# A masked graph layer: bf16 in three parts on 96 rows, and float32r in two parts on 32-row tiles

## The chip, the cores and the metric

The kernel runs on one core of a Trainium2 chip. A core has TensorE (PE, the matrix engine), VectorE (DVE), ScalarE (ACT), GpSimd (POOL) and SyncE (SP, which here only issues transfers). Each has its own queue of instructions and works it off in order; semaphores tie them together. TensorE multiplies a stationary operand (loaded first, "LDWEIGHTS" or PEld) with a moving one that is streamed column by column, and leaves the sums in PSUM, a memory of eight banks with 512 float32 columns in each of 128 partitions. The other engines read PSUM ("drain" it) and work in SBUF. The metric is device time in microseconds; lower is better.

## The reference

There are 128 graphs of 128 nodes with 64 features, and for each graph an adjacency matrix that is mostly zero (about 12% of its entries are positive, the diagonal among them).

```
h   = max(layernorm(x), 0)
mask = adj > 0
hm[j] = sum over k with mask[j,k] of relu(h[j] @ W1a + (h[j] - h[k]) @ W1b + b1)   # 192 units
x   = x + hm @ W2 + deg * b2
h   = max(layernorm(x), 0)
x   = x + (adj @ h) @ W.T
```

The heavy part is the sum over neighbours. It splits into a node part and a centre part: relu(c[k] + a[j]) with c = -h @ W1b and a = h @ (W1a + W1b) + b1. Only the pairs (j, k) that the mask allows count.

## The kernel before

**Groups.** The graphs are worked off in 32 groups of four (`G = 4`). For a group, `pre_...` functions prepare, `Job`s do the slot products, and `edge_...`, `slot_sum` and `post0` to `post4` finish. While the jobs of group g run, the preparation of group g+1 and the finish of group g-1 are put between them.

**Slots.** The 128 nodes k are cut into four quarters (`Q = 4`) of 32. In each quarter a centre j gets up to `D = 6` slots, one for each neighbour there; neighbours beyond that go to an overflow list of up to 128 edges per graph (`edge_x`, `edge_sum`, `edge_sum1`). `pre_rank` gives each neighbour its number in its quarter, and `pre_slots` makes the one-hot S: S[k, d, j] is 1 where k is slot d of j. A product of S with the node parts c puts c[k] into (d, j); a product of an identity with the centre parts adds a[j] to it. Unused slots then hold relu(a[j]) alone, which the term z takes off again.

**Parts.** `pre_proj` projects two graphs at a time into PSUM (float32 products into the tile `pp`, with a bf16 product for the biases) and splits the result exactly into three bf16 parts: ScalarE copies the first (`ca<-pp`), VectorE subtracts (`rest`), ScalarE copies the second (`ca<-rest`), POOL subtracts for the third. A slot product has to add the three parts, so they are stacked: `pre_stack` copies each quarter's 32 rows of each part to 96 rows (k3, twelve copies of 96 KB), and S is copied to three times 32 rows as well (S3, twelve copies of 192 KB at the end of `pre_slots`). In group 0 S3 is made in place by `first_ranks` and `first_slots`.

**Jobs.** A `Job` takes one double bank of PSUM (`gtile`, a pool of three double banks; `pre_proj` takes its `pp` from the same pool; the small tiles have the other two banks). It handles two quarters for one half (64) of the centres. Kind 0, called wide here, handles units 0 to 127 of one graph: two node products of 384 columns and four centre products of 192. Kind 1, called narrow, handles units 128 to 191 of two graphs, 64 rows of output for each, and so twice as many products on half the array. There are 16 wide and 8 narrow jobs in a group. The drain of a wide job is one VectorE reduction (`hm<-g`, sum of absolute values over slots); a narrow one is a Relu on ScalarE (`T<-g`) and additions on POOL.

**Order.** TensorE's order is the program's (`mm` and `tp` keep it; they are lines 181 and 184 in the profile): job by job, and behind each job the pieces that the tables OWN, BEHIND and AHEAD name for it. The other engines' instructions go through a wrapper (line 198) that holds the program order only until the main loop; there the framework's scheduler orders them by its own priorities. Every copy between partitions is issued on SP.

Of the kernel before, what the change touches and what calls it, by code (L numbers as in the profile page):

```python
# [9 lines left out]
BF16 = mybir.dt.bfloat16  # L10
I32 = mybir.dt.int32
# [139 lines left out]
def kernel(  # L151
# [67 lines left out]
    K3 = 3 * QN  # L219
# [8 lines left out]
    with ExitStack() as main:  # L228
# [41 lines left out]
        triq = const.tile([P, P], BF16, tag="triq", name="triq")  # L270
        vec.memset(triq, 0.0)
# [3 lines left out]

        triq3 = tmp.tile([P, Q, 3, QN], BF16, tag="u0", name="triq3", bufs=1)
        for part in range(3):
            vec.tensor_copy(
                triq3[:, :, part], triq.rearrange("p (q j) -> p q j", q=Q)
            )  # L280
# [5 lines left out]

        rks = const.tile([P, D, G * N], BF16, tag="rks", name="rks")
        for i in range(D):
            pool.memset(rks[:, i], float(i) + BIG)

        mident = const.tile([P, P], F32, tag="mident", name="mident")
        identb = const.tile([P, P], BF16, tag="identb", name="identb")

        id32 = const.tile([P, QN], F32, tag="id32", name="id32")
        id3 = const.tile([P, QN], BF16, tag="id3", name="id3")
# [3 lines left out]
        def constants():  # L299
            vec.tensor_scalar(mident, ident, -1.0, None, ALU.mult)  # L300
            vec.tensor_copy(identb, ident)
            vec.tensor_reduce(
                id32, ident.rearrange("p (q j) -> p j q", q=Q), AX.X, ALU.add
            )
            vec.tensor_copy(id3, id32)
            vec.tensor_copy(upb, upper)
            vec.tensor_scalar(ioe, iov, BIG, None, ALU.add)
# [13 lines left out]

        def weight_loads():
            act.dma_start(w2a, W2[0:C0, :])
            act.dma_start(b1c, b1[0:C0].unsqueeze(1))
            act.dma_start(bias[:, 0:H], b1.unsqueeze(0).to_broadcast([P, H]))
            act.dma_start(b2s, b2.unsqueeze(0).to_broadcast([P, O]))
            for p in range(2):
                s = slice(p * F, (p + 1) * F)
                sp.dma_start(w1[s], W1.rearrange("(t f) h -> f t h", t=2))
# [16 lines left out]
        def weights_b():  # L346
# [3 lines left out]
            pw = mtile("pw")  # L350
            tp(pw[:, 0:P], wab[:, 0:C0], ident)
            vec.tensor_tensor(bias[:, H : H + O], pb[:, 0:O], b2s, ALU.add)
            vec.tensor_scalar(wp[:, 0:H], w1[:, 1], -1.0, None, ALU.mult)
            vec.tensor_copy(wT, pw[:, 0:P])
# [27 lines left out]
        groups: dict[int, dict] = {}  # L382

# [38 lines left out]
        def pre_adj(g):  # L422
# [8 lines left out]
            d["maskT"] = grp.tile([P, G, N], BF16, tag="maskT", name=f"maskT{g}")  # L431
# [23 lines left out]
        def pre_slots(g, first, last):  # L455

            d = groups[g]
            if first == 0:
                d["S"] = one.tile([P, D, G * N], BF16, tag="S", name=f"S{g}")
            n = last - first  # L460
            vec.tensor_tensor(
                d["S"][:, first:last], bc(d["qs"].rearrange("k b j -> k (b j)"), n, 1),
                rks[:, first:last], ALU.is_equal,
            )
            if last < D:
                return
            d["S3"] = grp.tile([K3, Q, D, G * N], BF16, tag="S3", name=f"S3{g}")
            for q in range(Q):
                for part in range(3):
                    sp.dma_start(  # L470
                        d["S3"][part * QN : (part + 1) * QN, q],
                        d["S"][q * QN : (q + 1) * QN],
                    )

        def first_ranks(g, qp):

            d = groups[g]
            pk = gtile(f"pk{g}_{qp}")
            if qp == 0:
                d["q3"] = tmp.tile([K3, Q, G * N], BF16, tag="T", name=f"q3{g}", bufs=3)  # L480
            for i in range(2):
                q = 2 * qp + i
                mm(
                    pk[0:K3, i], triq3[:, q].rearrange("k t j -> k (t j)"),
                    d["maskT"].rearrange("k b j -> k (b j)"), start=True, stop=True,
                )
            act.activation(d["q3"][:, 2 * qp : 2 * qp + 2], pk[0:K3], AF.Copy)

        def first_slots(g, q):

            d = groups[g]
            if "S3" not in d:
# [534 lines left out]
```

## Time and profile before

| | |
|---|---|
| runs | 1012.18, 1013.48, 1016.25 us, median 1013.48 |
| profiled execution | span 1013.2 us; no time of its own is listed beside the span |
| TensorE busy, weight loads busy | 963.8 us (95%), 721.6 us (71%) |
| VectorE, ScalarE, POOL busy | 799.7 us (79%), 704.1 us (69%), 765.9 us (76%) |
| granted TensorE clock, mean | 0.980 |
| DMA | 129.94 MB, 128 GB/s in the mean |
| S copies / k copies | 372 of 192 KB / 384 of 96 KB |

The page gives each engine's busy time in the span and then groups of instructions by line, engine and tile: busy time in all, the mean of one in ns, and the idle time just before them with what ended it. A tile's name stands for all its buffers: g is a job's double bank, S the one-hot, k the stacked parts, id the identity, hm and T the drains' results, pp the projection, pe and px the overflow edges. Because matmuls overlap in the pipeline, the time between the starts of two of them says more than their durations. The view of TensorE in order of time merges neighbours of the same kind ("x4") and gives start, length from the first start to the last end, and what they are.

### The profile page before, as it was taken

The numbers are of one execution on the slowest core, as the hardware profiler recorded it, in microseconds if no ns is written. First come the engines' busy times: TensorE is split into PE (matmuls) and PEld (weight loads), VectorE is DVE, ScalarE is ACT, GpSimd is POOL, SyncE is SP. The second block draws the span as 40 slices with busy tenths as digits, with TensorE's granted clock in tenths as the row PEclk, the third lists the DMA queues.
The fourth block names the chain that finished last, engine by engine and source line by source line (L and its number), as shares of the span: only waits on it lengthen the run. The fifth ranks groups of instructions, "written<-read, shape, count | busy, mean of one in ns | idle before, by whom it ended". The sixth has DMA issues, their size and how long they took to land.

```text
span 1013.2 us, 27270 instructions
## 1 busy us (share of the span) xinstructions
PE 963.8 (95%) x10314; PEld 721.6 (71%) x10314; DVE 799.7 (79%) x1769; ACT 704.1 (69%) x1732; POOL 765.9 (76%) x1134
## 2 busy tenths in 40 slices
PE   3899999999999999999999999999999999999996
PEld 2577777777777777777777777777767777777774
DVE  7767888777888877788877788877787877788863
ACT  5557876677777667777667787667786667787652
POOL 3278777787877777877778877777877778877783
PEclk9599999999999999999999999999999999999998
DMA  3526655556755556766555766545765555765420
GB/s 83 133 68 162 147 135 130 123 124 154 161 136 134 122 120 140 163 136 138 126 123 129 162 144 136 131 112 128 162 140 133 127 120 132 162 147 119 110 67 14
DMA packets 88296, 129.94 MB, mean 128 GB/s; under 512 B 47200, under 2 KB 63968, under 8 KB 88160
## 3 DMA queue, kind: packets, MB, share of 16 engines
q1 hardware_dynamic: 87584, 127.98, 55.2%
q8 instruction: 83, 1.36, 0.5%
q14 instruction: 53, 0.43, 0.1%
q10 hardware_dynamic: 576, 0.16, 0.1%
HBM read 13.01 MB, written 4.19 MB: 17 GB/s over the span
## 4 chain that ended last, share of the span: by engine, by line
PE 45%; DVE 25%; ACT 14%; DMA 5%; POOL 4%; issue 3%; SPq 2%; DVEq 1%; POOLq 0%; ACTq 0%
PE g L181 24%; DVE hm L198 9%; PE pe L181 8%; DVE S L198 8%; DMA k<-ca 4%; ACT ca L198 3%; PE px L181 3%; DVE u L198 3%; ACT et L198 3%; POOL T L198 3%; SPq L198 2%; PE pp L181 2%; PE py L181 2%; ACT h L198 2%; ACT T L198 2%
## 5 line engine op out<-in xcount | busy, mean ns | idle before, releaser
L198 POOL TENSOR_TENSOR T<-T 128x192 f32<-128x192 f32 (+2 forms) x768 | 543.6, 714 | 139.0 <-ACT T L198 99.1
L181 PEld LDWEIGHTS <-k 96*128 96x128 bf16 (+1 forms) x6144 | 412.4, 104 | 208.5 <-issue 87.4
L198 DVE TENSOR_REDUCE hm<-g 128x64 f32<-128x768 f32 x512 | 472.1, 948 | 110.4 <-PE g L181 108.6
L181 PE MATMUL g<-S,k 96*128 96x384 bf16 (+1 forms) x2048 | 392.1, 333 | 29.2 <-DMA k<-ca 14.3
L181 PE MATMUL g<-id,k 96*128 96x192 bf16 (+1 forms) x4096 | 384.1, 248 | 0.0
L198 ACT ACTIVATE T<-g 128x768 f32<-128x768 f32 x256 | 209.8, 821 | 48.5 <-PE g L181 48.5
L198 POOL TENSOR_TENSOR ca<-rest,ca 128x384 bf16<-128x384 f32 x126 | 114.0, 924 | 82.3 <-ACT ca L198 72.0
L198 ACT ACTIVATE ca<-pp 128x768 bf16<-128x768 f32 x64 | 51.3, 802 | 63.9 <-PE pp L181 63.9
L198 DVE TENSOR_TENSOR S<-qs,rks 128x1024 bf16<-128x1024 bf16 x93 | 86.9, 962 | 0.1
L198 ACT ACTIVATE hT<-ph 128x256 f32<-128x256 f32 x32 | 12.3, 383 | 104.0 <-PE ph L184 104.0
L181 PE MATMUL pe<-RT,X 128*64 128x128 f32 (+1 forms) x512 | 74.9, 285 | 0.0
L181 PE MATMUL pe<-mident,z 128*64 128x128 f32 (+1 forms) x512 | 68.8, 274 | 0.0
L181 PE MATMUL pp<-wp,hT 64*128 64x448 f32 x256 | 68.7, 614 | 0.0
L198 ACT ACTIVATE z<-pp,ns 128x128 f32<-128x128 f32 (+1 forms) x256 | 65.7, 347 | 0.0
L198 ACT ACTIVATE ca<-rest 128x768 bf16<-128x768 f32 x64 | 55.2, 863 | 11.6 <-DVE rest L198 11.6
L198 DVE TENSOR_TENSOR rest<-pp,ca 128x768 f32<-128x768 f32 x64 | 60.7, 948 | 3.2 <-ACT ca L198 3.1
L198 DVE TENSOR_SCALAR maskT<-adjT 128x512 bf16<-128x512 f32 x32 | 17.2, 538 | 52.7 <-PE pe L181 52.7
L198 ACT ACTIVATE et<-et,half 128x128 f32<-128x128 f32 x128 | 56.8, 449 | 0.0
L181 PEld LDWEIGHTS pe<-mident,z 128*64 128x64 f32 (+1 forms) x512 | 53.8, 164 | 0.0
L181 PEld LDWEIGHTS pe<-RT,X 128*64 128x64 f32 (+1 forms) x512 | 52.8, 164 | 0.1
L181 PE MATMUL px<-ca,S 128*128 128x192 bf16 x384 | 52.7, 246 | 0.0
L181 PE MATMUL px<-ca,R 128*128 128x192 bf16 x384 | 52.6, 246 | 0.0
(128 smaller groups left out, 1263.1 us busy)
## 6 DMA issues: line engine op xcount, KB each, us to landing
S<-S SPq DMA_DIRECT2D x372, 192.0 KB, 4.0
k<-ca SPq DMA_DIRECT2D x384, 96.0 KB, 2.2
adj<-in_adj_dram SPq DMA_DIRECT2D x32, 256.0 KB, 3.0
x<-in_x_dram SPq DMA_DIRECT2D x32, 128.0 KB, 2.7
out_dram<-ot SPq DMA_DIRECT2D x32, 128.0 KB, 2.2
w<-in_L_gnn_W_dram SPq DMA_DIRECT2D x2, 96.0 KB, 5.1
bias<-in_L_gnn_b_dram ACTq DMA_DIRECT2D x1, 96.0 KB, 4.6
w2a<-in_L_gnn_W_dram ACTq DMA_DIRECT2D x1, 32.0 KB, 2.2
```

Source lines behind the costliest of these rows:

```text
L181: return tc.keep_in_program_order(nc.tensor.matmul(*args, **kw))
L198: ins = f(*args, **kw)
```

## The change

The projection is split in two float32r parts in place of three bf16 parts. float32r is a 4-byte form of float32 with a shorter mantissa. ScalarE copies the first part (once for the node half, once for the centre half) and VectorE's subtraction writes the second; the third part on POOL and the second copy on ScalarE go. The parts lie in two tiles `cas` that the groups use in turn, each with a block of zeros between the two graphs' node parts, so that a window of 128 columns holds one graph's narrow units beside zeros.

The slot products read the node parts and S where they lie: 32 rows of a quarter as one tile of TensorE, four quarters one after the other into four different banks. A job now takes two double banks and all four quarters; there are 8 wide and 4 narrow jobs in a group. Each part has its own product. A narrow job makes two passes over the nodes, one for each graph's window. Only the centre parts are copied: `ar` holds, on each quarter's 32 rows, the centre parts of every quarter w (sixteen copies of 192 KB on SP).

S, the mask, R, S2 and qj become float32r. S is made by six comparisons with a number each, and the table `rks` goes. The special treatment of group 0 and of the last group's order goes. The tables have twelve places instead of 24.

```diff
             def fill(self):
-                d = groups[self.g]
-                j0 = self.jh * JH
-                for i in range(2):
-                    q = 2 * self.qp + i
-                    for b, us, rows in self.parts:
-                        mm(
-                            self.cols(rows, i), d["k3"][:, q, 0, b, us],
-                            d["S3"][:, q, :, b * N + j0 : b * N + j0 + JH],
-                            start=True, stop=False, skip_group_check=True,
-                        )
...
+                rounds = [(self.nodes, n) for n in range(1 + self.kind)]
+                rounds += [(self.centres, v) for v in range(2)]
+                for f, n in rounds:
+                    for part in range(2):
+                        for q in range(Q):
+                            f(q, n, part)
...
+                self.gt = [gtile(f"g{g}_{kind}_{b}_{jh}_{i}") for i in range(2)]
...
+            def nodes(self, q, n, part):
+                g, b = self.g, self.b
+                if self.kind == 0:
+                    c = ca_of(g, part, 0, b, K0)
                 else:
+                    c = window(g, part, b, (LOWER, UPPER)[n])
+                j0 = (b + 2 * n) * N + self.jh * JH
+                mm(
+                    self.bank(q), c[ROWS[q]], groups[g]["S"][ROWS[q], :, j0 : j0 + JH],
+                    start=n + part == 0, stop=False, skip_group_check=True,
+                )
...
+                    groups[g]["ar"][ROWS[q], 2 * self.jh + v, part, r, a : a + P],
+                    bc(id32r[ROWS[q]], D, 1),
...
         def pre_stack(g):
+            d["ar"] = grp.tile([P, Q, 2, 2, 2 * H], F32R, tag="ar", name=f"ar{g}")
+            for w in range(Q):
+                for q in range(Q):
+                    sp.dma_start(
+                        d["ar"][ROWS[q], w].bitcast(F32),
+                        cas[g % 2][ROWS[w], :, :, CA:CW].bitcast(F32),
+                    )
...
         def pre_slots
+            for i in range(first, last):
+                vec.tensor_scalar(
+                    d["S"][:, i], d["qs"].rearrange("k b j -> k (b j)"), float(i) + BIG, None,
+                    ALU.is_equal,
+                )
...
         def pre_proj
-            act.activation(parts[0], x, AF.Copy)
+            for t in range(2):
+                act.activation(part(0, t), x[:, :, t], AF.Copy)
...
-            vec.tensor_tensor(rest, x, parts[0], ALU.subtract)
-            second()
-            third(pool)
+            for t in range(2):
+                vec.tensor_tensor(part(1, t), x[:, :, t], part(0, t), ALU.subtract)
...
         AHEAD = {
             0: (pre_adj,),
+            1: (pre_norm, pre_hT, pre_rank),
+            2: (lambda g: pre_slots(g, 0, 3), pre_count),
+            3: (lambda g: pre_slots(g, 3, D), lambda g: pre_proj(g, 0),),
+            4: (pre_edge_a,),
+            6: (lambda g: pre_proj(g, 1), pre_stack),
+            9: (pre_edge_b, pre_place),
+            10: (pre_edge_c,),
+            11: (pre_edge_d,),
         }
+        OWN: edge_x in 7 and 8
+        BEHIND: slot_sum 0, edge_sum 1, edge_sum1 2, post0 4, post1 5, post2 7, post3 8, post4 10
...
         for r in range(2):
+            for s in range(2):
+                ORDER += [(0, 2 * s + r, 0), (0, 2 * s + r, 1), (1, r, s)]
```

(The last two lines of the tables are shortened to the functions' places.)

## The prediction, made before the result was known

> **What bounds the kernel now.** I read the page's first two parts, then the groups by shape, TensorE's order of time over one group, and last SyncE and the table by stretches. All numbers are microseconds of the profiled execution unless marked.
>
> ```profile
> span 1013.2 us, 27270 instructions
> ...
> PE 963.8 (95%) x10314; PEld 721.6 (71%) x10314; DVE 799.7 (79%) x1769; ACT 704.1 (69%) x1732; POOL 765.9 (76%) x1134
> ```
>
> TensorE is busy without a break and nothing else is over 79%. The groups say what it is busy with and whom it waits for (busy, mean ns | idle before, releaser):
>
> ```profile
> L198 DVE TENSOR_REDUCE hm<-g 128x64 f32<-128x768 f32 x512 | 472.1, 948 | 110.4 <-PE g L181 108.6
> L181 PE MATMUL g<-S,k 96*128 96x384 bf16 x1024 | 261.4, 330 | 29.2 <-DMA k<-ca 14.3 <-DVE hm L198 12.7 <-DVE S L198 0.9
> L181 PEld LDWEIGHTS pe<-mident,z 128*128 128x128 f32 x256 | 38.9, 192 | 0.0
> ```
>
> VectorE waits 108.6 for TensorE's slot products; TensorE waits only 12.7 for VectorE's drains: three double banks, one per job, let TensorE run two jobs ahead. Now TensorE in order of time (start, length, work):
>
> ```profile
> 500.25 0.17 PE L181 MATMUL pv<-nb,upb 128*128 128x4 bf16 x1
> ...
> 503.05 1.02 PE L181 MATMUL pp<-wp,hT 64*128 64x448 f32 x4
> 503.91 0.28 PE L181 MATMUL pp<-biasp,oneb 64*128 64x256 bf16 x2
> ...
> 508.21 0.52 PE L181 MATMUL g<-S,k 96*64 96x384 bf16 x4
> 508.56 0.50 PE L181 MATMUL g<-id,k 96*64 96x192 bf16 x8
> 508.89 0.61 PE L181 MATMUL pga<-adjT,h 128*64 128x128 f32 x8
> ...
> 510.09 0.50 PE L181 MATMUL g<-S,k 96*128 96x384 bf16 x2
> 510.43 0.49 PE L181 MATMUL g<-id,k 96*128 96x192 bf16 x4
> 510.76 0.49 PE L181 MATMUL g<-S,k 96*128 96x384 bf16 x2
> ...
> 516.53 0.60 PE L184 MATMUL pt<-ident,adj 128*128 128x128 f32 x4
> 516.97 0.62 PE L181 MATMUL g<-S,k 96*128 96x384 bf16 x2
> ...
> 530.16 0.17 PE L181 MATMUL pv<-nb,upb 128*128 128x4 bf16 x1
> ```
>
> From start to start: one group takes 530.16 - 500.25 = 29.9. A wide job is 510.76 - 510.09 = 0.67 (two node products at 0.17, four of the centres at 0.083), a narrow one 0.68. So 24 jobs are 16.2 of a group, and the other matrix work with small waits is 13.7. SyncE, and a stretch of ten microseconds (busy time of PE, weight loads, DVE, ACT and POOL, then TensorE's granted clock, the DMA engines' busy share, and GB/s):
>
> ```profile
> 499.26 7.54 SPq L198 DMA_DIRECT2D S<-S  x8
> 506.90 8.74 SPq L198 DMA_DIRECT2D k<-ca  x12
> ```
> ```profile
> 498.00:508.00 10.00, 10.00 (x99) 7.11 (x97) 9.71 (x30) 9.36 (x30) 7.56 (x14) 1.00 0.99 211
> ```
>
> While S is copied the DMA engines are full (share 0.99) at 211 GB/s: eight copies of 192 KB in 7.54, or 0.94 each. That is the row for the new copies, which have the same size.
>
> **The change, part by part.**
>
> *TensorE's slot products.* Per group there are 8 wide and 4 narrow jobs of double size. A wide one has 2 rounds of nodes (384 columns) and 4 of centres (192), each round four 32-row tiles side by side; a narrow one has 4 and 4. No row shows float32r, so I bound it: bf16 takes 0.17 for 384 columns; a float32 product is issued as two instructions (pp shows x4 for two calls) and a pair of 64-row tiles with 448 columns takes 0.43, 0.96 ns a column, so 384 columns are 0.37. The Trainium skill (FP8 and Floating Point Precision, TensorE Precision Notes) says that true FP32 makes four passes and names a reduced reading of FP32 apart from it. The rows agree on the four (two instructions at twice bf16's time); the single pass no run here shows. I take 0.17, since float32r leaves out just what the other passes add; the transposes, one instruction each and still 0.11 for 128 columns, speak against it, and that end is rival B. A round of 192 columns is set by its weight load: float32 products with 128 weights follow each other by 0.11 (pt: 0.44 for four). So a wide job is 2 x 0.17 + 4 x 0.11 = 0.78, a narrow one 4 x 0.17 + 4 x 0.11 = 1.12, a group 8 x 0.78 + 4 x 1.12 = 10.7 in place of 16.2.
>
> That four tiles run side by side is an extension of pp: its two tiles' four instructions take 0.86, where one after the other, at twice bf16's 0.43 ns a column, they would take 1.5. The skill (TensorE: Matmul & The Clock Gate, Measured speedup vs the span model) has 3.07 times, not 4, for four row tiles. By that a node round is 4 x 0.17 / 3.07 = 0.22, a group +1.6, the whole +50. I go by the row (nearly full overlap) and keep 50 for the range.
>
> *The new coupling.* A job now takes two of the three double banks (`Job.__init__`, `gtile`). Its round order touches the second bank pair with the third product, and that one is free only when the job before has had its first drain. After a wide job this window is 0.17 (a 192-column product ends 0.25 after it starts, 0.08 of it stream) + 0.95 (drain) + about 0.1 (two semaphores) = 1.2; after a narrow one, with ScalarE's 0.82, 1.1. Per group 8 x 1.2 + 4 x 1.1 = 14.0. Other matrix work hides in it; where a window's pieces are longer, they count: behind job 1 edge_sum (2.66 before; eight float32r at 0.11 for twelve bf16 at 0.056 gives 2.9), the hT transposes and ranks, 3.4 in all, +2.2; behind jobs 2, 4 and 8 +0.5. Sum 16.7. pre_proj takes a double bank too, twice: the next job then needs both drains (+0.9), and the one after it waits until ScalarE and VectorE have emptied pp (+0.3): 2.3. Entering and leaving the tile mode costs about 0.1 (528.21, the last product's start, to 528.38 at py, against 0.08) where no window covers it: 0.8. Together 10.7 + 16.7 + 2.3 + 0.8 = 30.5, and 1 for VectorE's other work queued ahead of a drain: **31.5** against 29.9.
>
> *Copies.* Twelve S copies (192 KB) and twelve k copies (96 KB) go; sixteen ar copies of 192 KB come (32 rows x 6 KB). The bytes fall from 3.5 to 3.1 MB a group, but all now stand behind pre_proj(1) and ahead of job 1, whose centres read the last eight (`2 * jh + v`); before, the S copies were earlier. On TensorE, from job 1's centres to the end of pp in job 6 lie: 0.44, 3.4, 1.1, 1.3, 0.8, 2.1, 0.8, 1.6, 1.1, 1.1, 0.8, 1.2 = 15.7. From there the copies go: ScalarE's part and VectorE's subtraction behind a drain or two, 3.0 (before: pp done at 504.2, the subtraction at 507.8); 16 x 0.94 = 15.0; the last landing about 1.5 more. Total 15.7 + 19.5 = 35.2. A row sends 1.5 KB pieces here, not 6 KB; k's 3 KB packets took 189 ns each against 457, 16 GB/s an engine instead of 13, and with that a copy is 0.75 and the loop 32.2. I take **33** (nearer to the quick end, because waits lengthen the loop's other side less than they hide): the end of job 1 waits, and job 2 and edge_sum, in order behind it, wait too.
>
> *The rest costs nothing,* hidden under TensorE's loop. VectorE keeps 16 drains of 0.95 a group; six S comparisons at about 0.54 (the row of maskT, 538 ns) replace three of 0.96; the subtraction is split in two. ScalarE loses the second part (55.2 in all) and gains a split copy; POOL loses the third part (114.0) and adds in fewer pieces. VectorE's 799.7 is 25.0 a group, under 33 with room; were its cover gone, the S comparisons' 0.4 and the splits' 0.2 a group would be 19 in all. The x, adj and out transfers stay in SP's queue; were adj behind the sixteen copies and late, the transposes in job 0 would wait, but a load is issued a group ahead.
>
> *Ends.* Group 0's copies are 16 x 0.94 instead of 12 in 9.98: +5. The last job is a narrow one, whose ScalarE and POOL sums stand ahead of edge_sum1: +2.
>
> **Sum.** 1013.2 + 31 x (33 - 29.9) + 7 = 1116, rounded to 1115. The span agrees with the median 1013.48 to 0.03%, so nothing is added for what lies around it.
>
> **Rivals.**
> A, the forecast: the loop through the ar copies sets 31.3 to 35: 1050 to 1175.
> B, float32r streams at the float32 rate, 2.2 times: jobs 1.3 and 2.0 (8 x 1.3 + 4 x 2.0 = 18.4), period 31.5 + 7.7 = 39, copies hidden under it: 1013 + 31 x 9.1 + 7 = 1300. For it: the 0.11 of the float32 transposes. Against: a float32 product needs two instructions for its precision, float32r gives that up.
> C, the other side: the copies land in time and TensorE's relief is collected. Period 10.7 + 16.7 = 27.4, 1013 - 31 x 2.5 + 7 = 943. It decides once the way from pp's end to the last landing is under 29.9 - 15.7 = 14.2, that is (14.2 - 4.5) / 16 = 0.61 a copy, 322 GB/s. For it: a k copy was issued every 0.59 (but 96 KB). Against: 211 GB/s with full engines.
> D, coupling, copies and relief cancel: a period of 29.5 to 30.5, 1000 to 1035.
>
> **How the numbers follow.** A 0.60, B 0.19, C 0.14, D 0.07. A measurement here tells about 0.5% from no change (1008.4 to 1018.5); a third of D lies in it, with a tail of A, 0.03; a quarter of D is faster: 0.16; slower 0.81. A's own range is 1050 to 1175. For 8 in 10 I leave out the lower two thirds of C and the upper half of B: 985 to 1300.
>
> **What would show it.** Right: TensorE's busy share falls to some 75%; g waits for DVE hm rise from 12.7 to over 100; waits of g for DMA ar some 2 to 4 per group, in the second wide job. A node round of four at 0.17 and a centre round at 0.11 confirm the fills; 0.35 and 0.2 are B. Wrong: no wait for ar at all, or a period under 29.9, would mean that copies move faster than 0.61 each, or that the drains release TensorE sooner than 1.2 after a job.

## The result, and the profile after

| | before | after |
|---|---|---|
| median of the runs, us | 1012.83 (1009.80 to 1016.25) | 1624.01 (1620.95 to 1626.26) |
| profiled execution: span, own time | 1013.2, not listed | 1621.4, 1623.33 |
| granted TensorE clock, mean | 0.980 | 0.757 |
| one group, median between the first products of pv | 30.0 | 49.1 |

The kernel is slower by 611, a ratio of 1.602 (95% interval 1.597 to 1.608). The direction was forecast, the size was not: 1115 was forecast, and the time lies far outside 985 to 1300.

The page of the kernel after: the span, busy time by engine, the granted clock in 40 slices (in tenths), and the shares of the chain that ended last.

```profile
span 1621.4 us, 33949 instructions
...
PE 1321.0 (81%) x14023; PEld 1028.0 (63%) x14023; DVE 826.8 (51%) x1925; ACT 680.2 (42%) x1730; POOL 588.6 (36%) x748
...
PEclk7578777788768678777786667887877776777776
...
SPq 27%; PE 25%; ACT 22%; DVE 10%; DMA 9%; issue 5%; POOL 2%; ACTq 0%; DVEq 0%; POOLq 0%
```

No engine is near its limit, and TensorE's 1321 busy microseconds are stretched by a clock that is at half for about half of the time (791.6 us in the records of the clock, which show full and half speed and nothing between). The chain goes round through SP, TensorE, ScalarE and VectorE. The groups by shape of the kernel after (busy, mean ns | idle time before, releasers):

```profile
L199 DVE TENSOR_REDUCE hm<-g 128x64 f32<-128x768 f32 x512 | 465.2, 950 | 351.3 <-PE g L182 351.3
...
L182 PE MATMUL g<-S,ca 32*128 32x384 f32 x4096 | 445.1, 445 | 190.6 <-DVE hm L199 88.4 <-ACT T L199 85.2 <-DVE ca L199 10.8
L182 PE MATMUL g<-id32r,ar 32*128 32x192 f32 x6144 | 379.1, 312 | 74.7 <-DMA ar<-ca 72.7
...
L199 DVE SCALAR_TENSOR_TENSOR mrb<-mvb,rsb 128x4 f32<-128x4 f32 x32 | 45.2, 1412 | 0.1
```

TensorE now waits for both drains (88.4 for VectorE's, 85.2 for ScalarE's; before, 12.7 and nothing) and for the copies (72.7). The last row, a product of 4 columns, takes 1412 ns; it comes back below, beside its row of before. TensorE in order of time over one group of the kernel after (779.78 to 828.03, 48.2):

```profile
785.17 0.98 PE L182 MATMUL g<-S,ca 32*128 32x384 f32 x16
785.96 0.61 PE L182 MATMUL g<-id32r,ar 32*128 32x192 f32 x16
786.50 0.66 PE L182 MATMUL pe<-RT,X 128*64 128x128 f32 x8
...
788.18 0.63 PE L182 MATMUL g<-S,ca 32*128 32x384 f32 x8
788.64 0.59 PE L182 MATMUL g<-id32r,ar 32*128 32x192 f32 x16
789.16 1.02 PE L182 MATMUL pp<-wp,hT 64*128 64x448 f32 x4
...
799.43 1.01 PE L182 MATMUL g<-S,ca 32*128 32x384 f32 x6 [2.79 <-ACT T L199]
...
801.17 1.86 PE L182 MATMUL pp<-wp,hT 64*128 64x448 f32 x4
...
805.05 0.69 PE L182 MATMUL g<-S,ca 32*128 32x384 f32 x2 [1.81 <-DVE hm L199]
...
827.37 0.74 PE L182 MATMUL g<-id32r,ar 32*128 32x192 f32 x5 [1.11 <-DMA ar<-ca]
```

At 785.17 stands a narrow fill, 1.33 from start to start, at 788.18 a wide one, 0.98. Job 6 waits 2.79 in the middle of its fill, job 7 waits 1.81. Between them the four float32 products of pp take 1.86; at 789.16 the same four took 1.02: the clock has gone to half. The end of job 1, at 822 to 828, waits for ar. What ScalarE, VectorE and POOL do while job 6 and job 7 wait, in order of time:

```profile
795.49 1.28 ACT L199 ACTIVATE et<-iov,mid 128x128 f32<-128x128 f32 x4 [1.67 <-DVE mid L199]
...
796.67 1.26 ACT L199 ACTIVATE et<-et,half 128x128 f32<-128x128 f32 x4
...
797.96 0.72 ACT L199 ACTIVATE R<-et,ones 128x512 fp32r<-128x512 f32 x1
798.59 1.49 ACT L199 ACTIVATE T<-g 128x768 f32<-128x768 f32 x2
...
800.16 3.95 POOL L199 TENSOR_TENSOR T<-T 128x768 f32<-128x768 f32 x4 [7.52 <-ACT T L199]
...
800.52 1.47 DVE L199 SCALAR_TENSOR_TENSOR mrb<-mvb,rsb 128x4 f32<-128x4 f32 x1
...
803.37 0.28 ACT L199 ACTIVATE sda<-mva,eps 128x4 f32<-128x4 f32 x1
...
804.05 1.81 DVE L199 TENSOR_REDUCE hm<-g 128x64 f32<-128x768 f32 x2
```

The drain T, for which job 6 waits, stands behind nine instructions for et and R (3.2 together). The drain hm, for which job 7 waits, stands behind the norm of two groups, which goes back and forth between the engines: mrb, then four Relus on ScalarE, sda, rsa, mra. And the clock in stretches of two microseconds (busy time of PE, weight loads, DVE, ACT, POOL, then the clock, DMA share, GB/s):

```profile
798.00:800.00 2.00, 0.57 (x8) 0.57 (x12) 0.14 (x2) 2.00 (x4) 0.00 (x0) 0.50 0.00 0
...
806.00:808.00 2.00, 2.00 (x24) 1.83 (x24) 0.29 (x1) 1.67 (x7) 0.25 (x1) 0.50 0.00 0
```

It falls with the wait and stays at half while TensorE is busy again. Last, SP in the same group:

```profile
808.51 0.37 SPq L199 DMA_DIRECT2D x<-in_x_dram  x1
808.98 14.69 SPq L199 DMA_DIRECT2D ar<-ca  x16
```

The sixteen copies are issued in 14.69, or 0.92 each, but the first only 5.8 after pp's last product (803.2); the last lands at 827.4, 3.7 behind its issue.

### The profile page after: what moved, and what is told of

Same layout as the page of the kernel before. It is cut to its first block, busy times and chain, and to the rows that moved or that the text cites. A ratio compares the mean times of both kernels' runs of the same rounds, so it can differ in the third digit from the quotient of the medians.

```text
span 1621.4 us, 33949 instructions
## 1 busy us (share of the span) xinstructions
PE 1321.0 (81%) x14023; PEld 1028.0 (63%) x14023; DVE 826.8 (51%) x1925; ACT 680.2 (42%) x1730; POOL 588.6 (36%) x748
## 4 chain that ended last, share of the span: by engine, by line
SPq 27%; PE 25%; ACT 22%; DVE 10%; DMA 9%; issue 5%; POOL 2%; ACTq 0%; DVEq 0%; POOLq 0%
SPq L199 27%; PE pe L182 11%; DMA ar<-ca 9%; PE g L182 7%; ACT h L199 5%; ACT et L199 5%; ACT z L199 4%; DVE hm L199 3%; ACT T L199 3%; DVE mrb L199 3%; PE pp L182 2%; ACT ca L199 2%; ACT e L199 2%; DVE ca L199 1%; PE pd L182 1%
## 5 line engine op out<-in xcount | busy, mean ns | idle before, releaser
L199 POOL TENSOR_TENSOR T<-T 128x768 f32<-128x768 f32 (+3 forms) x512 | 475.9, 930 | 769.5 <-ACT T L199 739.4
L182 PE MATMUL g<-S,ca 32*128 32x384 f32 x4096 | 445.1, 445 | 190.6 <-DVE hm L199 88.4
L182 PEld LDWEIGHTS g<-S,ca 32*128 32x128 f32 x4096 | 242.1, 219 | 348.6 <-DVE hm L199 180.8
L182 PE MATMUL g<-id32r,ar 32*128 32x192 f32 x6144 | 379.1, 312 | 74.7 <-DMA ar<-ca 72.7
L182 PEld LDWEIGHTS g<-id32r,ar 32*128 32x128 f32 x6144 | 359.6, 230 | 101.9 <-DMA ar<-ca 100.6
L199 DVE TENSOR_TENSOR ca<-pp,ca 128x384 fp32r<-128x384 f32 x128 | 65.4, 552 | 109.0 <-ACT e L199 109.0
L182 PE MATMUL px<-ca,S 128*128 128x192 f32 x256 | 83.5, 425 | 0.0
L182 PE MATMUL pe<-maskT,ca 128*128 128x128 f32 x256 | 78.3, 403 | 0.0
L182 PE MATMUL px<-ca,R 128*128 128x192 f32 x256 | 75.6, 393 | 0.0
L199 DVE TENSOR_SCALAR S<-qs 128x512 fp32r<-128x512 bf16 x192 | 67.6, 422 | 0.0
```

The lines of the kernel that those rows point to most:

```text
L182: return tc.keep_in_program_order(nc.tensor.matmul(*args, **kw))
L199: ins = f(*args, **kw)
```

## The experiments

The expectations number their explanations. Theory 1: the loop through the copies of ar, as forecast, only longer, and its wait pulls the clock down. Theory 2: the coupling of a job to two of the three double banks makes TensorE wait for the drains. Beside them stood the granted clock by itself. Theory 3 came after the first four runs: the drains are late because they stand behind other work on ScalarE and VectorE. All times are medians, beside a median of 1013 to 1016 for the kernel before in the same series.

**Copies by halves.** The copies are cut by r and go out after each of the two pre_proj, jobs 3 and 6, so that half of them are three jobs earlier.

```diff
-        def pre_stack(g):
+        def pre_stack(g, r):
...
-                        d["ar"][ROWS[q], w].bitcast(F32),
-                        cas[g % 2][ROWS[w], :, :, CA:CW].bitcast(F32),
+                        d["ar"][ROWS[q], w, :, r].bitcast(F32),
+                        cas[g % 2][ROWS[w], :, r, CA:CW].bitcast(F32),
...
-            3: (lambda g: pre_slots(g, 3, D), lambda g: pre_proj(g, 0),),
+            3: (..., lambda g: pre_proj(g, 0), lambda g: pre_stack(g, 0)),
-            6: (lambda g: pre_proj(g, 1), pre_stack),
+            6: (lambda g: pre_proj(g, 1), lambda g: pre_stack(g, 1)),
```

> The change with its sixteen ar copies of 192 KB cut into two lots of sixteen of 96 KB: the lot of the first half (r = 0, which jobs 0 to 5 read) right behind pre_proj(0) in job 3, the other (read from job 6 on) behind pre_proj(1). Computes everything. Theory 1 (the late copies close the loop, and their wait of 5 us a group in job 1 makes TensorE's clock fall): no wait of g for ar is left, the clock goes to over 0.95, the period from 48.2 to about 34, the time to 1150 +- 60. Theory 2 (the drains' coupling makes the waits and the half clock; the copies only fill a wait): the 5 us go and nothing else, period 43, 1450 to 1500, clock under 0.85.

Measured: 1430.84, ratio 1.412 (1.388 to 1.435), clock 0.789. The groups by shape of this kernel:

```profile
L182 PE MATMUL g<-S,ca 32*128 32x384 f32 x4096 | 443.9, 445 | 190.4 <-DVE hm L199 87.7 <-ACT T L199 85.7 <-DVE ca L199 10.6
L182 PE MATMUL g<-id32r,ar 32*128 32x192 f32 x6144 | 330.2, 307 | 0.8
```

The wait for ar is gone, and 193 with it, 6 a group. The waits for the drains are what they were, and so are 418 of the 611. The loop through the copies is real, but it is a third of the loss. Of the two readings the second is the nearer one, though its 1450 to 1500 was just missed.

**No copies.** From the third group on, no copy of ar is issued, and the jobs read what the first groups left.

```diff
+            d["ar"] = ars[g % 2]
+            if g > 1:
+                return
```

> The change without the ar copies of groups 2 to 31 (they read what groups 0 and 1 left; the copies are left out, and with them the right centre parts). Theory 1: as when the copies come early, 1150 +- 60, clock over 0.95. Theory 2: 1450 to 1500. If this one is clearly faster than the run with copies in two lots, the copies also cost by their traffic or their place in SyncE's queue.

Measured: 1443.32, ratio 1.424 (1.408 to 1.441): not below the run with early copies. The copies cost what they are late, and their traffic nothing that these runs can tell.

**Kept warm.** The kernel after, with bf16 products of 512 columns whose results nobody reads, 20 in job 1 before its centres, 10 ahead of job 6, 8 ahead of job 7.

```diff
+        def warm(n, name):
+            pm = mtile(name)
+            for i in range(n):
+                mm(pm, oneb, warmb, start=True, stop=True)
```

> The change with idle matrix work added where TensorE waits in every group from the second on: 20 products of 512 bf16 columns (4.3 us at full clock) between nodes and centres of job 1, ten before job 6, eight before job 7. Waits as before, only the clock is held. Theory of the clock (half the time goes at half clock, and that is why the pieces and fills between job 1 and job 6 take 23.4 us and not 15.7): clock over 0.95, period down by 5 to 8 us, 1380 to 1470. If the clock is only a sign of waiting and the waits take up what the faster work saves, no change: 1600 to 1660, and slower if the added work is not covered.

Measured: 1584.04, ratio 1.563 (1.545 to 1.581), clock 0.904. The clock is mostly held, and 40 come back, near the second reading. By itself the clock is not the limit of this kernel. The idle products are busy for 274 us where TensorE waited before; what they cost themselves was not measured.

**Two tiles at a time.** The fill does all rounds for quarters 0 and 1, then for 2 and 3, so that its second double bank is touched only in the second half.

```diff
-                for f, n in rounds:
-                    for part in range(2):
-                        for q in range(Q):
-                            f(q, n, part)
+                for h in range(2):
+                    for f, n in rounds:
+                        for part in range(2):
+                            for q in (2 * h, 2 * h + 1):
+                                f(q, n, part)
```

> The change with a job's rounds taken for quarters 0 and 1 first and then for 2 and 3: two 32-row tiles side by side in place of four, and the second double bank is touched only in the second half of the job, so that no job waits for the first drain of the one before. Fills grow from 13 to about 21 us a group. Theory 2 (coupling): waits of g for hm and T fall from 276 to under 60 in all, clock up, under 1350 in spite of the longer fills. Theory 1 (copies): the copies' loop stays with its 24 us from pp to the last landing and an opposite side that is no shorter, 1450 to 1620.

Measured: 1886.83, clock 0.62. The groups by shape, and stretches of four microseconds:

```profile
L182 PE MATMUL g<-S,ca 32*128 32x384 f32 x4096 | 753.4, 508 | 83.5 <-ACT T L199 51.1 <-DVE ca L199 20.7 <-DVE hm L199 4.6
```
```profile
952.00:956.00 4.00, 4.00 (x32) 3.76 (x30) 2.25 (x3) 0.30 (x1) 0.65 (x1) 0.50 0.96 195
956.00:960.00 4.00, 4.00 (x34) 3.78 (x33) 0.00 (x0) 1.41 (x3) 0.08 (x1) 0.50 0.79 158
```

The wait for hm falls from 88.4 to 4.6, as the coupling would have it, but two tiles side by side take so long that TensorE becomes the bound, at a clock that stays at half although TensorE is busy all the time (the slices shown; it is so from 936 to 968). The time lies above both readings. As a test of the coupling the run says little; what it shows of the clock stands at the end.

**Program order.** VectorE and ScalarE are held in the order of the program, so that nothing is moved ahead of a drain; once in the kernel after, once with the copies by halves.

```diff
-                return tc.keep_in_program_order(ins) if Engine.held else ins
+                return tc.keep_in_program_order(ins) if Engine.held or self.always else ins
```

> The change with VectorE's and ScalarE's instructions held in the program's order in the main loop too, so that a drain stands right behind its job and ahead of the pieces named after it; copies late as in the change. Theory 3 (the drains are late because other work of their engine was put ahead of them: 3 us of et and R ahead of the narrow drain of job 5, the norm's chain ahead of the wide drain of job 6; the idle time halves the clock from job 6 to job 8): the waits in jobs 6 and 7 (2.8 and 1.8 us) go, the side from job 1 to pp shortens from 23.4 to about 17, 1350 to 1450. Theory 2 (one double bank too few, whatever the order): waits of g for hm and T stay over 150 in all, 1550 to 1650.

> Both: copies in two lots and VectorE and ScalarE in program order. Theory 3: no long wait is left in a group, the clock stays up, the period falls from 41.7 to 32 to 35, 1070 to 1180, the time that the prediction's sum had without copies. Theory 2: 1380 to 1440, as with the copies alone.

Measured: 1762.06 and 1557.62, each worse than the same kernel with the free order (1624.01 and 1430.84), and above every range that was expected. Whom TensorE waits for with both changes (us in total, times, the longest):

```profile
PE ph L185 <- ACT h L200: 153.0, 30, 5.1
PE g L182 <- DVE hm L200: 106.7, 104, 2.6
```

The waits for ScalarE's drains go (85.7 to 4.0 with the copies by halves), those for hm rise (87.7 to 106.7), and h comes late: a new wait of 153, 5 a group. So this order removes one wait and brings another; a choice of order that avoids the wait for h is tried below.

**Early copies and warm.** The copies by halves, with idle products ahead of jobs 6 (10) and 7 (8).

> Copies in two lots, and idle matrix work of ten and eight products of 512 bf16 columns ahead of jobs 6 and 7, where TensorE waits 2.8 and 1.8 us; the drains stay late. It measures the clock's share by itself: jobs 6 to 8 run at half clock for about 11 us of a group; held at full clock they should save 4 to 5 of the 41.7, 1270 to 1310, with the clock over 0.95. If the late drains alone matter, no gain: 1410 to 1450.

Measured: 1439.40, clock 0.897, against 1430.84 and 0.789 without: no gain that two runs of each can tell. While the drains set the pace, a faster clock only makes room for waiting: the waits of g (142.8) and the idle products (busy for 130.9) are 274 together, where the waits were 190.4.

**The coupling alone.** The kernel before, its bf16 products as they are, but two neighbouring jobs are filled together, node rounds of both and then centre rounds of both, and drained together: a step takes two of the three double banks. The pieces between jobs then stand behind both jobs of a pair, and the first and the last group lose their special order.

```diff
+        def fill_two(two):
+            for job in two:
+                job.nodes()
+            for w in range(2):
+                for job in two:
+                    job.centres(w)
...
-                job = Job(g, *args)
-                job.fill()
-                job.drain()
+                if t % 2 == 0:
+                    two = [Job(g, *a) for a in order[t : t + 2]]
+                    fill_two(two)
+                    for job in two:
+                        job.drain()
```

> The kernel before with one thing of the change: two neighbouring jobs are filled together, so that each step takes two of the three double banks (all node products of both, then all centre products, then both drains; the job order of the middle groups in every group). bf16, 96 rows and the copies stay. If the coupling is what costs: fills 16.2 + windows and pieces 16.7 + pp's 2.3 = 35 a group in place of 29.9, 1150 to 1250, waits of g for hm and T over 150 in all, and the clock under 0.95 where the waits exceed 2 us. If the coupling is harmless and the change is slow for its own products or order, under 1040.

Measured: 1118.71, ratio 1.103 (1.097 to 1.109), clock 0.985, a group every 33.4. The groups by shape of this kernel:

```profile
L181 PE MATMUL g<-S,k 96*128 96x384 bf16 x1024 | 238.4, 328 | 84.6 <-ACT T L198 34.1 <-DVE hm L198 29.6 <-DMA k<-ca 11.5
```

The coupling, with the pieces moved behind the pairs, costs 105 even where nothing else of the change is made, the clock is full and ScalarE and VectorE have about the loads of before (703 and 813 busy). This is the mechanism that the forecast priced as windows of 1.2. The expectation took it at 35 a group, 5 more than before, with waits over 150; measured are 3.4 more and waits of 63.7, so it is real and was priced too high for this kernel.

**Relief in one place.** The copies by halves; pre_edge_a moves from job 4 to job 9, and the subtraction goes ahead of z and e.

```diff
-            4: (pre_edge_a,),
-            9: (pre_edge_b, pre_place),
+            9: (pre_edge_a, pre_edge_b, pre_place),
...
-            zs()
-            es()
             for t in range(2):
                 vec.tensor_tensor(part(1, t), x[:, :, t], part(0, t), ALU.subtract)
+            zs()
+            es()
```

> Copies in two lots, and the queues ahead of the late drains relieved: pre_edge_a (nine ScalarE operations, 3.2 us with pre_edge_b, which stood ahead of job 5's drain) moves from job 4 to job 9, and VectorE's subtraction stands ahead of z and e. If ScalarE's queue is what holds job 6: its 2.8 us wait goes, the clock does not fall there, the period drops from 41.7 to 34 to 37, 1190 to 1280. If the wait is only handed on to the next chain (the norm's, on VectorE), 1380 to 1440.

Measured: 1467.71, ratio 1.447 (1.438 to 1.456). The groups by shape of this kernel:

```profile
L182 PE MATMUL g<-S,ca 32*128 32x384 f32 x4096 | 429.3, 468 | 154.7 <-DVE hm L199 129.8 <-ACT e L199 13.5 <-ACT T L199 7.6
```

The wait of g for T falls from 85.7 to 7.6, that for hm rises from 87.7 to 129.8. The wait is handed on to the next drain in line, as in the second reading, whose 1380 to 1440 was a little too low.

**Short drains.** The copies by halves; every drain reads two of the six slots.

```diff
-                            self.gt[n][:, :, 0:ND].rearrange("h i (d j) -> h j i d", d=D),
+                            self.gt[n][:, :, 0 : DR * JH].rearrange("h i (d j) -> h j i d", d=DR),
...
-                        self.gt[n][:, :, 0:ND].rearrange("h i (d j) -> h i d j", d=D),
+                        self.gt[n][:, :, 0 : DR * JH].rearrange("h i (d j) -> h i d j", d=DR),
...
-                for m in (2 * D, D, n):
+                for m in (2 * DR, DR):
```

> The copies go by halves as in the first experiment, and every drain reads only the first two of the six slots of each bank: VectorE's reductions and ScalarE's Relus take 256 elements in place of 768, some 0.40 in place of 0.95 and some 0.40 in place of 0.82, and POOL adds less (the sum over the other four slots is left out). Nothing else is shortened. If TensorE waits for the length of the drains (the window of 1.2 behind each job), 12 windows a group lose some 0.5 each, 6 a group: period 41.7 - 6 = 36, 1230 to 1270. If it waits for what is queued ahead of the drains on VectorE and ScalarE (the norm's chain, et and R, the pieces of pre_proj), the drains' own length matters only where no chain stands ahead: 2 a group or less, 1370 to 1430. Waits of g for DVE hm: under 40 by the first, still over 60 by the second.

Measured: 1360.05, ratio 1.341 (1.323 to 1.358), clock 0.747. Neither number: 71 less, where one reading said 160 to 200 and the other up to 60. By its sign, the waits for hm, the first reading came true (3.9, under 40), so the drains' own length counts. The groups by shape, and two stretches:

```profile
L182 PE MATMUL g<-S,ca 32*128 32x384 f32 x4096 | 408.3, 469 | 106.8 <-DVE ca L199 51.5 <-ACT T L199 46.6 <-DVE hm L199 3.9
```
```profile
710.00:712.00 2.00, 2.00 (x12) 1.78 (x8) 0.73 (x2) 1.24 (x6) 0.69 (x1) 0.50 0.67 157
...
716.00:718.00 2.00, 2.00 (x14) 1.56 (x12) 0.00 (x0) 0.55 (x2) 1.27 (x3) 0.50 0.70 160
```

The waits for hm go from 87.7 to 3.9, those for T from 85.7 to 46.6, and 51.5 appear for pp's subtraction. TensorE is 90% busy now, and for half of the time at half clock: the bound has changed from the drains to a slow TensorE. (POOL's adds are shorter too, and with them mrb: 323 ns in place of 1420. This belongs to the 71.)

**Short drains and warm.** The same, with idle products ahead of job 4 (5), job 6 (8) and job 7 (2).

> The experiment with short drains (copies by halves, four of the six slots of each bank left out of the sums), in which TensorE is 90% busy and half of a group's products run at a granted clock of 0.5, with idle products of 512 bf16 columns added in front of job 4 (5), job 6 (8) and job 7 (2), where TensorE waits 1.2, 1.8 and 0.5; their results are not used. If the clock is what limits that kernel (14 of its 38.9 a group run at half), it stays over 0.9 and the period falls by 5 to 7: 1130 to 1200. If the clock stays up and the time does not follow (the waits take the place, as in the experiment with warm products and whole drains), 1320 to 1370. If the clock stays near 0.75 with TensorE kept busy, its cause is not the idle stretches.

Measured: 1246.56, ratio 1.226 (1.221 to 1.231), clock 0.930: 114 less than with short drains alone, where the same means gave nothing with whole drains. The groups by shape of this kernel:

```profile
L182 PE MATMUL g<-S,ca 32*128 32x384 f32 x4096 | 345.9, 399 | 93.6 <-DVE ca L199 59.2 <-DVE hm L199 25.7 <-DVE S L199 3.6
```

The forecast of 1130 to 1200 was too low, since the waits do not go entirely. So the two causes cover each other:

| copies by halves, and | clock free | kept warm |
|---|---|---|
| whole drains | 1431 | 1439 |
| short drains | 1360 | 1247 |

**Some order.** The copies by halves; only the drains, the norm, et and R are held in program order, and the norm stands behind job 0, hT behind job 2.

```diff
-            0: (pre_adj,),
-            1: (pre_norm, pre_hT, pre_rank),
+            0: (pre_adj, pre_norm),
+            1: (pre_rank,),
-            2: (lambda g: pre_slots(g, 0, 3), pre_count),
+            2: (pre_hT, lambda g: pre_slots(g, 0, 3), pre_count),
```

> The copies go by halves as in the first experiment; the drains, the norm's pieces, et and R alone are held in the order of the program, the norm of the next group stands behind job 0 and hT behind job 2, so that no norm and no et or R is moved ahead of a drain by the planner. If what was hoisted ahead of the drains is the cause of the rest, the waits of 2.8 and 1.8 before jobs 6 and 7 go and the period falls from 41.7 by 4 to 7: 1190 to 1310. If the order is not what counts (the same pieces must pass through the same engines between the same drains, in whatever order), the waits reappear elsewhere and the time is 1400 to 1470, as in the experiments on order before.

Measured: 1436.44 (one value, without an interval) against 1430.84. The second reading holds by this one value: no choice of order that was tried beats the free one.

**One part.** Of the 1247 with short drains and a warm clock, 233 above the kernel before were left. Here each job also leaves out the products of the second parts.

```diff
-                    for part in range(2):
+                    for part in range(1):
```

> The experiment with short drains and warm products (copies by halves; four of six slots of each bank left out of the sums; idle products ahead of jobs 4, 6 and 7), and now every job issues only the products of the first parts: 8 rounds a group fewer... the wide fill has 1 round of nodes and 2 of centres in place of 2 and 4, the narrow 2 and 2 in place of 4 and 4, so the remainders' part of the slot products is left out; parts are still made and copied. A wide fill took 0.98 and a narrow 1.33, so a group's fills fall from 13.2 to some 6.8. If the 233 that is left over before is TensorE's own fills, the period falls from 35.9 by 5 to 6.4: 1045 to 1095. If it is the chain through ScalarE and VectorE around pre_proj, TensorE only waits longer: 1170 to 1240.

Measured: 1223.64, ratio 1.205 (1.199 to 1.210), clock 0.820. Half of all fills go and 23 come back, so TensorE only waits longer, as in the second reading. But the test is not clean, because the clock falls with the work (at half for 442 us in place of 176), and TensorE's busy time falls by 83 only (1116.6 to 1033.3); what half of the fills is worth at a held clock was not measured. TensorE, and ScalarE with VectorE, in order of time in this kernel:

```profile
642.58 0.77 PE L182 MATMUL g<-S,ca 32*128 32x384 f32 x4 [1.47 <-DVE hm L199]
...
646.93 1.25 PE L182 MATMUL g<-S,ca 32*128 32x384 f32 x8 [2.31 <-DVE ca L199]
```
```profile
640.16 1.43 ACT L199 ACTIVATE h<-x,mrb,rsb 128x64 f32<-128x64 f32 x4 [0.67 <-DVE mrb L199]
...
642.22 1.44 ACT L199 ACTIVATE h<-x,mra,rsa 128x64 f32<-128x64 f32 x4 [0.44 <-DVE mra L199]
...
643.56 0.84 ACT L199 ACTIVATE ca<-pp 128x384 fp32r<-128x384 f32 x2
644.30 1.01 ACT L199 ACTIVATE z<-pp,ns 128x128 f32<-128x128 f32 x4
645.19 0.54 ACT L199 ACTIVATE e<-pp,dn 128x64 f32<-128x64 f32 x2
...
645.76 1.02 DVE L199 TENSOR_TENSOR ca<-pp,ca 128x384 fp32r<-128x384 f32 x2 [2.91 <-ACT e L199]
```

From the norm to the subtraction ScalarE has one chain with short stops, and jobs 7 and 8 stand at its links: pp holds a double bank until the subtraction is done, and job 8 needs it. Fills that end sooner wait for these links.

**Short norm.** Whole fills again, short drains, warm; each normalisation is one Relu of 256 elements in place of four of 64.

```diff
-            for b in range(G):
-                act.activation(
-                    to(b), src[:, b, :], AF.Relu, bias=mr[:, b : b + 1], scale=rs[:, b : b + 1]
-                )
+            act.activation(
+                to, src.rearrange("p b f -> p (b f)"), AF.Relu, bias=mr[:, 0:1], scale=rs[:, 0:1]
+            )
```

> The experiment with short drains and warm products (fills whole again, in two parts), and each of the two normalisations of a group is one instruction of ScalarE over 256 elements in place of four over 64 (some 0.35 in place of 1.43; the scale and shift of three of the four matrices are left out, so these matrices are normalised with those of the first). ScalarE's chain from the drain of job 5 to the subtraction of pre_proj(1) gets shorter by 2 x 1.08 = 2.2 and nothing of TensorE's work changes. If this chain is what is left, TensorE's waits in front of jobs 7 and 8 (0.9 and 1.9) go, the period falls by 1.5 to 2.5, and 1246 becomes 1165 to 1200. If TensorE's own work is what is left, the time stays within 1230 to 1250.

Measured: 1177.45, ratio 1.164 (1.153 to 1.175), clock 0.949: 69 less, as much as the expectation said, for 2.2 of ScalarE's work a group. The groups by shape of this kernel:

```profile
L182 PE MATMUL g<-S,ca 32*128 32x384 f32 x4096 | 335.9, 389 | 45.0 <-DVE ca L199 34.9 <-DVE S L199 3.9 <-DVE hm L199 0.8
```

The waits of g have gone from 93.6 (short drains, warm) to 45.0. So the chain through ScalarE is shown to be a part of the rest. The 162 that still lie above the kernel before were not split further. The idle products are busy for 116 us here; how much of that stands where TensorE would otherwise wait is not shown.

## Why the prediction was right and wrong

**The failed step** is the end of the coupling's sum, "and 1 for VectorE's other work queued ahead of a drain", with "The rest costs nothing" behind it. The forecast saw that a job now takes two of three double banks, priced the drain itself (a window of 1.2 behind each job), and then took VectorE's and ScalarE's other work as hidden, because their busy time was far below the period. But with this coupling a drain is on TensorE's path, and so is whatever stands ahead of it on its engine. In the trace job 6 waits 2.79 behind et and R, job 7 1.81 behind two norms; over the span the waits for hm and T are 174, or 5.6 a group. By the forecast's sum a kernel without the copies' loop would have a period of 31.5 and take 1013 + 31 x 1.6 + 7 = 1070; with the copies early or gone it takes 1431 and 1443. Undoing one wait (the order, pre_edge_a) handed it to the next drain; cutting the drains with the clock held took 184, and cutting 2.2 of the norm another 69. The 184 holds three things that were not separated: the drains' own length, POOL's shorter additions, and with these the shorter mrb. So it is shown that the path through the drains sets the pace, and that the norm ahead of them is a part of it; the share of the queue in the 184 is read from the trace and not measured. VectorE's 25.0 of work in a period of 33 told nothing of it. Of the forecast's signs the waits for hm came near (88.4, over 100 was said), the waits for T were not foreseen, and TensorE's share is 81%, not 75%.

**The clock** was not in the sum: every duration was taken from rows at 0.98. Each group now has two stops, job 6 to 7 and the end of job 1, and the clock is at half for half of the time. The Trainium skill (TensorE: Matmul & The Clock Gate, HAM oscillation — how this bites in real kernels) has the mechanism: a wait in each turn of a loop that empties a window of some 3.4 us throttles the next turn, every turn anew. It agrees with the trace in kind, but here a window need not be empty: the wait of job 6 lasted 2.79, and the clock fell when 1.3 of it had passed. In the records of the clock of the kernel after, all changes lie 3.41 us or a multiple of it apart; in the 3.41 ahead of its 64 falls, two a group, TensorE was still busy for 18 to 79%, and ahead of its 64 returns for 88 to 100%. The price of the half clock depends on what else bounds: nothing or 40 with whole drains, 114 with short ones. A forecast that sees such a wait enter every turn of a loop has to ask for the clock too.

**The fills.** A wide one takes 0.98 where 0.78 was forecast, a narrow one 1.33 in place of 1.12: 13.2 a group in place of 10.7. A round of four tiles with 384 columns takes 0.23 (0.46 for two, 788.18 to 788.64), one with 192 columns 0.13 (0.52 for four). The rule that was weighed and set aside, the Trainium skill's 3.07 (TensorE: Matmul & The Clock Gate, Measured speedup vs the span model), gave 0.22 and is the nearer one; the row of pp, two tiles side by side, did not carry over to four. The single pass for float32r fits that number, and rival B's 0.35 is out. The error is 2.5 a group, at most 78 over the span; how much of it reached the time was not measured.

**The copies.** 0.94 each was forecast and 0.92 measured. The two ends of the loop were off: the first issue came 5.8 after pp and not 3.0 (the subtraction waits for ca, z and e on ScalarE, which wait for the norm), and the last landing 3.7 after its issue, not 1.5. So the copies' side is 24.2 in place of 19.5; the other side, from job 1's centres to pp in job 6, is 23.4 in place of 15.7, by the waits and the clock just told. The whole loop is 47.6 where 35.2 was worked out, and the choice of 33 at the quick end went the wrong way: the pieces of 1.5 KB took 115 ns each, which is 13 GB/s an engine, the rate of S's 6 KB before, and not the 16 of k's 3 KB. The mechanism holds: the end of job 1 waits for ar, 72.7 over the span or 2.3 a group, where 2 to 4 were named as the sign.

**The coupling** as such was right in kind: on the kernel before it adds 3.4 a group by itself (33.4 against 30.0).

**The ends.** 7 was forecast; it is 41. The first pv product stands at 42.8 (30.2 before), and from the last one to the end it is 86.5 (57.8 before): the first and the last group have the same waits and less beside them to hide in.

**The rivals.** B, C and D are out. C's condition, copies of 0.61, was asked of the wrong place: with early copies, and even without copies, the time is 1431 and 1443, not 943. C's period of 27.4 also left out three terms of the forecast's own sum (2.3, 0.8 and 1); with them it is 31.5, and by that sum no copy, however fast, would have made the kernel quicker. B was added up too low: its own 0.35 and 0.2 make jobs of 1.5 and 2.2, a period of 41.6 and 1383, not 1300. D's periods make 1008 to 1039, not 1000 to 1035. No case in the list had the drains of both engines as the bound, and so the range ended at 1300.

## What to carry to other kernels

When a step takes away a spare buffer, price not only the drain that it now waits for but also the queue in front of that drain: list what stands ahead of it on its engine, and what those instructions themselves wait for, whatever the busy share says. Then ask whether the new wait recurs in every turn of the loop and is long enough to drop TensorE's clock, because then the durations of TensorE that were read from the old trace can nearly double, as pp's 1.02 became 1.86. Two causes that cover each other must be removed together: here neither warm products nor short drains showed the 184 that both gave.

## What the runs showed of the hardware

- **Busy, and still at half.** With two 32-row tiles side by side, and px, pga and other short products between the fills, TensorE was busy almost without a gap from 936 to 968 and the clock stayed at 0.50; it came back only during edge_sum, a row of products on the whole array, most of them float32. With four tiles and short drains it stayed at half for 13 us of nearly unbroken work (705.5 to 719) before it came back. Busy time in the profile is not all that the clock follows; what else it follows these runs do not tell.
- **A small VectorE instruction beside POOL.** The 4-column product mrb took 292 ns before (its row follows), 1353 to 1420 in six kernels where it ran beside POOL's addition of 128x768 (1.81 us; 1113 in a seventh), and 323 to 370 where that addition was cut to 128x256. In the kernel after it ended 10 to 30 ns behind the POOL instruction that was running when it began, in 31 of 32 cases; the one that had no POOL instruction beside it took 161. So it waited for POOL's instruction to end. It stands in the middle of the norm's chain, so its microsecond counts.

```profile
L198 DVE SCALAR_TENSOR_TENSOR mrb<-mvb,rsb 128x4 f32<-128x4 f32 x32 | 9.3, 292 | 0.1
```

- **Four 32-row tiles in float32r.** A round of 384 columns took 0.23 and one of 192 columns 0.13, where the same kernel's two-tile float32 products (448 columns, two instructions each) took 0.43.
